# Layer 1's feed-forward: norm, stores, flips and the products of gate and up, regrouped

## The chip, the cores and the metric

The kernel runs on one core of a Trainium2 chip. The metric is the device time of one execution in microseconds (us). The engines are named as in the profile: PE is TensorE, DVE is VectorE, ACT is ScalarE, POOL is GpSimd, and SP is SyncE, which issues the stores here. In the trace each engine runs its own instructions in the order in which the built program has them, and waits at an instruction whose inputs are not there yet.

## The reference

The whole is a decoder of two layers on x of 4 x 512 rows of 512 columns. Each layer has a self-attention, a cross-attention and a feed-forward, and each of the six is followed by a norm:

```python
def _layernorm(x, axis=-1, eps=1e-05):
    m = jnp.mean(x, axis=axis, keepdims=True)
    v = jnp.var(x, axis=axis, keepdims=True)
    return (x - m) / jnp.sqrt(v + eps)
```

The change concerns the last of the six, layer 1's feed-forward, with weights of three values and inputs quantised to 8 bits by row:

```python
def _quant_act(x):
    s = jnp.max(jnp.abs(x), axis=-1, keepdims=True) / 127.0 + EPS
    xq = jnp.clip(jnp.round(x / s), -128.0, 127.0)
    return (xq, s)

def _qlinear(x, w):
    wq, ws = _quant_weight(w)
    xq, xs = _quant_act(x)
    y = jnp.einsum('bsi,oi->bso', xq, wq)
    return y * xs * ws
gate = jax.nn.silu(_qlinear(x, w_gate))
up = _qlinear(x, w_up)
return _qlinear(gate * up, w_down)
...
x = _layernorm(x + _L1_ffn_ref(x, L1_ffn_w_gate, L1_ffn_w_up, L1_ffn_w_down), axis=-1)
```

The inner width is 2048. The output is the result of that last norm.

## The kernel before, in words

x stays in SBUF as 16 tiles X[0] to X[15] of 128 rows by 512 columns; four tiles are one batch. The stages follow each other, and the feed-forward of layer 1 (`l1_ffn`) is the last. Its weights have been quantised and loaded as bf16 in the stage before, which also gives the scales `sg`, `su` and `sd` of the three weights as columns of one value per row.

`pipelined` runs `first(t)` for a tile, and after it `second(t - 1)` for the tile before.

`first(t)` finds the row's largest value (L1391), makes its scale `s` and the inverse (L1392, L1394), scales and rounds by adding a large constant (L1395, on DVE) and takes the constant off again into bf16 (L1396, on ACT). `flipped` turns the 128 x 512 values by four PE transposes into one PSUM tile (L1402), which DVE copies to SBUF (L1403). Then, for four pieces of 512 inner columns, PE makes gate's and up's products (`mm`, L160: four matmuls each, into `ps_s` and `ps_m`), ACT applies Silu to gate's (L1420), and DVE multiplies by up's (L1421). This gives four tiles `h` of 128 x 512.

`second(t, h)` takes the maximum of each `h` (L1427) and of the four (L1428), makes scale and inverse (L1429, L1430), quantises each piece (L1433 on DVE, L1434 on ACT) into `hq`, flips it by four groups of four transposes with four DVE copies (L1403), multiplies by the down weights (16 matmuls of L160 into one PSUM tile), and adds the result to X[t] (L1441, on DVE, the "residual" below).

After the fourth tile of a batch, `layernorm` takes mean and variance of its four tiles (`tile_moments`, L219 and L220 on DVE), the inverse root by ACT's Sqrt and a DVE reciprocal (`table_roots`, L243, L244), normalises the four tiles (`normalise_tile`, L239 on DVE), and SP stores them (L1445). Sqrt and Silu are in different tables of ACT, so that each batch has two loads of a table (ACT_TABLE_LOAD on L243 and L1420).

`inverse_roots` (L227 to L234) is the other way to the inverse root: a first guess from the bits of the number and three Newton steps, 15 small operations on POOL. Before the change it serves three batches of the cross-attention before, for four tiles at once.

Nothing in this stage writes the order of instructions out by hand. A scheduler puts each engine's instructions in order when the program is built, within what data, buffers and priorities allow; so the order on an engine isn't that of the source, and two tiles are mixed on every engine. Buffers here: three PSUM tiles each for `ps_s` and `ps_m`, two for `ps_t`; four `tmp` in SBUF, shared by the quantised x and Silu's outputs; eight tiles of h, which is two rows of tiles; one `hq` and one `hqt`.

Of the kernel before, what the change touches and what calls it, by code (L numbers as in the profile page):

```python
# [10 lines left out]
BF16 = mybir.dt.bfloat16  # L11
I32 = mybir.dt.int32
AF = mybir.ActivationFunctionType
ALU = mybir.AluOpType
AX = mybir.AxisListType
PSUM = bass.MemoryType.PSUM

P = 128
# [10 lines left out]
LN_EPS = 1e-05  # L29
Q_EPS = 1e-05  # L30
MASK_NEG = -2.3819763e38
ROOT_GUESS = float(0x5F3759DF)
ROUND = 12582912.0
# [53 lines left out]
def decoder_kernel(ctx: ExitStack, tc: tile.TileContext, a: dict, out: bass.AP):  # L87
    nc = tc.nc
# [20 lines left out]
    V, A, G, PE = nc.vector, nc.scalar, nc.gpsimd, nc.tensor  # L109


    def act(tag, free, bufs=1, dtype=F32):
        return ap.tile([P, *free], dtype, tag=tag, name=tag, bufs=bufs)

    def tmp(dtype=F32):
        return tp.tile([P, 512], dtype, tag="tmp", name="tmp")

    def small(n, tag, bufs=2):
        return sp.tile([P, n], F32, tag=tag, name=tag, bufs=bufs)

    def prob(tag, free, bufs, dtype=F32):
        return pools["pp"].tile([P, *free], dtype, tag=tag, name=tag, bufs=bufs)

    def pss():
        return pools["ps_s"].tile([P, 512], F32, tag="s", name="ps_s")

    def pst(dtype=F32):
        if "ps_t" not in pools:
            return psm(dtype)
        return pools["ps_t"].tile([P, 512], dtype, tag="t", name="ps_t")  # L130

    def psm(dtype=F32):
        return pools["ps_m"].tile([P, 512], dtype, tag="m", name="ps_m")
# [16 lines left out]
    def tk(t):  # L150
        return slice(t * P, (t + 1) * P)
# [4 lines left out]
    def mm(ps, lhs, rhs):  # L156

        n = len(lhs)
        for i, (x, y) in enumerate(zip(lhs, rhs)):
            PE.matmul(ps, lhsT=x, rhs=y, start=(i == 0), stop=(i == n - 1))  # L160
# [29 lines left out]
    X = []  # L190
    for t in range(T // P):
        x = xp.tile([P, F], F32, tag=f"x{t}", name=f"x{t}")
# [18 lines left out]
    moments = {}  # L211

    def tile_moments(b, i):

        if i == 0:
            moments[b] = small(8, "mv"), small(4, "rstd")
        mv = moments[b][0]
        st = sp.tile([P, 6], F32, tag="bn", name="bn")
        V.bn_stats(st, X[4 * b + i])  # L219
        V.bn_aggr(mv[:, 2 * i:2 * i + 2], st)  # L220

    def inverse_roots(b):


        mv, y = moments[b]
        v, t = small(4, "var"), small(4, "newton")
        G.tensor_scalar(v, mv.rearrange("p (t s) -> p t s", s=2)[:, :, 1], LN_EPS, None, ALU.add)  # L227
        G.tensor_scalar(y.bitcast(I32), v.bitcast(I32), -0.5, ROOT_GUESS, ALU.mult, ALU.add)
        G.tensor_scalar(v, v, -0.5, None, ALU.mult)
        for _ in range(3):  # L230
            G.tensor_tensor(t, v, y, ALU.mult)
            G.tensor_tensor(t, t, y, ALU.mult)
            G.tensor_scalar(t, t, 1.5, None, ALU.add)
            G.tensor_tensor(y, y, t, ALU.mult)  # L234

    def normalise_tile(b, i):
        mv, rstd = moments[b]
        x = X[4 * b + i]
        V.tensor_scalar(x, x, mv[:, 2 * i:2 * i + 1], rstd[:, i:i + 1], ALU.subtract, ALU.mult)  # L239

    def table_roots(b):
        mv, rstd = moments[b]
        A.activation(rstd, mv.rearrange("p (t s) -> p t s", s=2)[:, :, 1], AF.Sqrt, bias=LN_EPS)  # L243
        V.reciprocal(rstd, rstd)  # L244

    def layernorm(b):
        for i in range(4):
            tile_moments(b, i)
        table_roots(b)
        for i in range(4):  # L250
            normalise_tile(b, i)
# [46 lines left out]
    def pipelined(heads, first, second):  # L298

        held = None  # L300
        for h in heads:
            got = first(h)
            if held is not None:
                second(*held)
            held = (h, got)
        second(*held)
# [8 lines left out]
    def chunks(w):  # L315
        return [w[:, k, :] for k in range(w.shape[1])]
# [764 lines left out]
    def l1_xattn():  # L1081
# [163 lines left out]
        def out_projection(b, t, half, part):  # L1245

            if part == 0:
                kept["ps"] = psm()
            ps, n = kept["ps"][:, :256], slice(256 * half, 256 * half + 256)
            for k in range(2 * part, 2 * part + 2):  # L1250
                PE.matmul(ps, lhsT=fts[b][k][:, tk(t)], rhs=st["wo"][:, k, n],  # L1251
                          start=(k == 0), stop=(k == 3))
            if part == 0:
                return
            x = X[4 * b + t][:, n]
            V.tensor_tensor(x, x, ps, ALU.add)
            if half == 1:
                tile_moments(b, t)
            if (t, half) == (3, 1):
                (table_roots if b == B - 1 else inverse_roots)(b)  # L1260
# [123 lines left out]
    def l1_ffn():  # L1384
        wg, sg = quant["L1_ffn_gateT"]
        wu, su = quant["L1_ffn_upT"]
        wd, sd = quant["L1_ffn_downT"]

        def quantize(x, scratch, xq, s):

            V.tensor_reduce(s, x, AX.X, ALU.max, apply_absolute_value=True)  # L1391
            V.tensor_scalar(s, s, 1.0 / 127.0, Q_EPS, ALU.mult, ALU.add)  # L1392
            inv = small(1, "one", 8)
            V.reciprocal(inv, s)  # L1394
            V.tensor_scalar(scratch, x, inv, ROUND, ALU.mult, ALU.add)  # L1395
            A.activation(xq, scratch, AF.Copy, bias=-ROUND)  # L1396

        def flipped(dst, src, n):
            for c in range(n // 4):
                pt = pst(BF16)  # L1400
                for i in range(4):
                    PE.transpose(pt[:, tk(i)], src[:, tk(4 * c + i)], identb)  # L1402
                V.tensor_copy(dst[:, 4 * c:4 * c + 4, :], pt.rearrange("p (k n) -> p k n", k=4))  # L1403

        def first(t):
            s = small(1, "one", 8)
            xq, xqt = tmp(BF16), prob("q", [4, P], 3, BF16)
            quantize(X[t], tmp(), xq, s)
            flipped(xqt, xq, 4)
            gs, us = small(1, "one", 8), small(1, "one", 8)  # L1410
            V.tensor_tensor(gs, s, sg, ALU.mult)
            V.tensor_tensor(us, s, su, ALU.mult)
            h = [prob("P", [512], 8) for _ in range(4)]
            for n in range(4):
                pg, pu = pss(), psm()
                nn = slice(512 * n, 512 * n + 512)
                mm(pg, chunks(xqt), [w[:, nn] for w in wg])
                mm(pu, chunks(xqt), [w[:, nn] for w in wu])
                g = tmp()
                A.activation(g, pg, AF.Silu, scale=gs)  # L1420
                V.scalar_tensor_tensor(h[n], pu, us, g, ALU.mult, ALU.mult)  # L1421
            return h

        def second(t, h):
            part, s, inv = small(4, "part4"), small(1, "one", 8), small(1, "one", 8)
            for n in range(4):
                V.tensor_reduce(part[:, n:n + 1], h[n], AX.X, ALU.max, apply_absolute_value=True)  # L1427
            V.tensor_reduce(s, part, AX.X, ALU.max)  # L1428
            V.tensor_scalar(s, s, 1.0 / 127.0, Q_EPS, ALU.mult, ALU.add)  # L1429
            V.reciprocal(inv, s)  # L1430
            hq = prob("v", [4, 512], 1, BF16)
            for n in range(4):
                V.tensor_scalar(h[n], h[n], inv, ROUND, ALU.mult, ALU.add)  # L1433
                A.activation(hq[:, n, :], h[n], AF.Copy, bias=-ROUND)  # L1434
            hqt = act("attnT", [16, P], dtype=BF16)
            flipped(hqt, hq.rearrange("p n c -> p (n c)"), 16)
            po = psm()
            mm(po, chunks(hqt), wd)
            ds = small(1, "one", 8)
            V.tensor_tensor(ds, s, sd, ALU.mult)  # L1440
            V.scalar_tensor_tensor(X[t], po, ds, X[t], ALU.mult, ALU.add)  # L1441
            if t % 4 == 3:
                layernorm(t // 4)
                for i in range(4):
                    nc.sync.dma_start(out[tk(t - 3 + i), :], X[t - 3 + i])  # L1445

        pipelined(range(T // P), first, second)

    l1_ffn()


# [49 lines left out]
```

## Time and profile before

| | us |
|---|---|
| median of 3 runs | 2916.74 (2912.76 to 2916.99) |
| the profiled execution, its time | 2925.97 |
| its span | 2924.2 |
| mean granted PE clock | 0.983 |
| PE busy | 2763.2 (94%) |
| DVE busy | 1757.1 (60%) |
| ACT busy | 1046.8 (36%) |
| POOL busy | 425.0 (15%) |
| the feed-forward of layer 1 | 2704.9 to 2924.2 |
| in it: PE, DVE, ACT, POOL busy | 190.27, 195.11, 98.94, 0.00 |

The span is one profiled execution. A row of the timeline has start, duration (for several merged instructions from the first one's start to the last one's end), engine, line, operation, output and input, and the number of instructions; in brackets the idle time before it and who ended it. A row of the groups has total busy time, mean duration in ns, and the idle time before. A row of the chain of waits has start and length of a piece of the path that ended last. A row of the engines' busy time in a stretch has the stretch, its length, then busy time (and instructions) of PE, PE's weight loads, DVE, ACT and POOL, and then the clock, the DMA engines' share and GB/s.

### The profile page before, as it was taken

Reading aid. Unit: us, or ns where it says so; the run is one execution under the profiler, and the core shown is the slowest. Engines: PE = TensorE matmul, PEld = TensorE weight load, DVE = VectorE, ACT = ScalarE, POOL = GpSimd, SP = SyncE. Lnnn points to the kernel's source line nnn. Section 1 sums busy time; section 2 is a strip of 40 time slices with the busy share of each in tenths; the row PEclk is TensorE's granted clock in tenths of the full one; section 3 lists DMA queues with packets and bytes.
Section 4 is the critical chain, followed back from the end, with each engine's and each line's share of the span. In section 5 each row is a group of like instructions: output and inputs, shape, how many; then the busy total and the mean of one; then the engine's idle time right before and its main releaser. Section 6 shows DMA issues by size and latency. Waiting matters only on the chain. (4 is left out here: it accounts for less than half of the span.)

```text
span 2924.2 us, 30438 instructions
## 1 busy us (share of the span) xinstructions
PE 2763.2 (94%) x11434; PEld 1347.8 (46%) x11434; DVE 1757.1 (60%) x3551; ACT 1046.8 (36%) x1929; POOL 425.0 (15%) x436
## 2 busy tenths in 40 slices
PE   8999999998998889999999999999999999998987
PEld 3444444565665345555555555553334334334443
DVE  4565564553111476767667666756656666565998
ACT  2333342333221122232233223234555554554443
POOL 3000000042002100111101101123333232211000
PEclk9999999999999899999999999999999999999999
DMA  9700000004322120000000001111111020010000
GB/s 386 278 15 1 15 4 27 23 29 137 101 85 97 35 87 1 1 0 1 1 1 1 1 0 44 58 47 38 56 55 58 37 86 27 12 51 1 15 15 30
DMA packets 61128, 142.76 MB, mean 49 GB/s; under 512 B 6537, under 2 KB 26010, under 8 KB 54818
## 3 DMA queue, kind: packets, MB, share of 16 engines
q1 hardware_dynamic: 54818, 123.80, 11.8%
q0 software_dynamic: 6144, 16.79, 1.6%
q8 instruction: 99, 1.62, 0.2%
q14 instruction: 67, 0.55, 0.1%
HBM read 84.73 MB, written 47.45 MB: 45 GB/s over the span
## 5 line engine op out<-in xcount | busy, mean ns | idle before, releaser
L1182 DVE TENSOR_REDUCE maxes<-ps_b 128x2 f32<-128x1024 f32 x256 | 312.6, 1223 | 212.0 <-PE ps_b L1194 113.8
L160 PE MATMUL ps_m<-w,attnT 128*128 128x512 f32 (+1 forms) x992 | 391.8, 547 | 9.7 <-DVE x L313 9.7
L1198 ACT ACTIVATE PT<-ps_b 128x1024 f32<-128x1024 f32 x256 | 260.3, 1023 | 237.0 <-PE ps_b L1194 236.9
L1178 PE MATMUL ps_b<-k,q 32*128 32x512 f32 x1024 | 287.0, 642 | 6.8 <-ACT PT L1198 6.8
L1194 PE MATMUL ps_b<-q,k 32*128 32x512 f32 x1024 | 285.5, 642 | 1.4 <-DVE maxes L1182 1.4
L933 PE MATMUL ps_m<-xT,w 128*128 128x512 f32 x512 | 261.4, 594 | 0.0
L313 DVE TENSOR_TENSOR x<-x,ps_m 128x512 f32<-128x512 f32 x128 | 87.8, 687 | 284.5 <-PE ps_m L160 257.1
L160 PEld LDWEIGHTS ps_m<-w,attnT 128*128 128x128 f32 x736 | 141.2, 195 | 177.3 <-issue 162.8
L950 ACT ACTIVATE P<-ps_s,nmax 128x512 f32<-128x512 f32 (+3 forms) x256 | 135.4, 529 | 234.9 <-DVE nmax L948 233.8
L946 PE MATMUL ps_s<-k,q 128*128 128x512 f32 (+3 forms) x512 | 183.3, 441 | 19.1 <-POOL q L906 17.4
L906 POOL TENSOR_TENSOR q<-tmp 128x512 f32<-128x512 f32 x64 | 82.0, 1281 | 765.8 <-DVE tmp L905 731.2
L978 PE MATMUL ps_m<-PT,v 128*128 128x512 f32 (+3 forms) x512 | 162.8, 441 | 4.0 <-DVE PT L966 4.0
L370 ACT ACTIVATE P<-ps_s,nmax 128x512 f32<-128x512 f32 x128 | 88.5, 693 | 203.5 <-DVE nmax L368 203.5
L957 DVE TENSOR_SCALAR P<-P,sums 128x512 f32<-128x512 f32 (+3 forms) x256 | 152.0, 594 | 5.3
L1178 PEld LDWEIGHTS ps_b<-k,q 32*128 32x128 f32 x1024 | 76.5, 183 | 155.2 <-issue 141.1
L160 PE MATMUL ps_m<-w,xT 128*128 128x512 f32 (+1 forms) x384 | 143.8, 530 | 3.4 <-DVE v L338 3.4
L1205 PE MATMUL ps_m<-PT,vv 128*32 128x512 f32 x1024 | 137.5, 609 | 7.5 <-ACT PT L1198 7.5
L963 PEld LDWEIGHTS ps_t<-kc,P 128*128 128x128 f32 x640 | 84.0, 141 | 121.3 <-issue 82.0
L978 PEld LDWEIGHTS ps_m<-PT,v 128*128 128x128 f32 x512 | 89.0, 190 | 106.1 <-issue 48.8
L348 PE MATMUL ps_m<-xT,w 128*128 128x512 f32 x256 | 122.3, 605 | 10.4 <-DMA w<-in_L_attn_Wq 10.4
L948 DVE TENSOR_REDUCE nmax<-ps_s 128x1 f32<-128x512 f32 (+3 forms) x256 | 125.5, 490 | 5.6
L947 DVE TENSOR_TENSOR ps_s<-ps_s,mask 128x128 f32<-128x128 f32 x256 | 75.1, 294 | 81.1 <-PE ps_s L946 78.9
(281 smaller groups left out, 4403.7 us busy)
## 6 DMA issues: line engine op xcount, KB each, us to landing
hidden<-w SPq DMA_DIRECT2D x16, 1024.0 KB, 16.7
result<-w SPq DMA_DIRECT2D x16, 1024.0 KB, 16.3
w<-in_L_ffn_gateT SPq DMA_DIRECT2D x8, 1024.0 KB, 4.8
tmp<-tmp POOLq DMA_DIRECT2D x64, 128.0 KB
w<-in_L_ffn_upT SPq DMA_DIRECT2D x8, 1024.0 KB, 4.8
w<-in_L_ffn_downT SPq DMA_DIRECT2D x8, 1024.0 KB, 5.5
w<-in_L_attn_Wqkv SPq DMA_DIRECT2D x6, 1024.0 KB, 8.9
w<-in_L_attn_Wo SPq DMA_DIRECT2D x5, 1024.0 KB, 13.6
```

Source lines behind the costliest of these rows:

```text
L160: PE.matmul(ps, lhsT=x, rhs=y, start=(i == 0), stop=(i == n - 1))
L933: PE.matmul(ps_q[n], lhsT=wq[h // 4][:, i, tk(h % 4)], rhs=st["xt"][:, i, :], start=(i == 0), stop=(i == 3))
L946: PE.matmul(s[:, :w], lhsT=q[:, tk(qi)], rhs=k[:, :w], start=True, stop=True)
L948: V.tensor_reduce(nmax[:, qi:qi + 1], s[:, :w], AX.X, ALU.max, negate=True)
L950: A.activation(p[:, :w], s[:, :w], AF.Exp, bias=nmax[:, qi:qi + 1], accum_out=sums[:, qi:qi + 1])
L957: V.tensor_scalar(p[:, :w], p[:, :w], sums[:, qi:qi + 1], None, ALU.mult)
L978: PE.matmul(av[:, c * P:], lhsT=st["v"][:, c, tk(g)], rhs=pts[c][:, c * P:], start=(c == 0), stop=(c == 3))
L1178: PE.matmul(s[:, j, :], lhsT=q[strip(i), tk(qi)], rhs=k[strip(i), :], start=True, stop=True)
L1182: V.tensor_reduce(at[:, 2 * half:2 * half + 2, 16 * (1 - g % 2)], s, AX.X, ALU.max, negate=True)
L1194: PE.matmul(s[:, j, :], lhsT=k[strip(i), tk(c)], rhs=q[strip(i), :], start=True, stop=True)
L1198: A.activation(p, s, AF.Exp)
L1205: PE.matmul(avs[g][strip(i), :], lhsT=vv[c][:, 4 * m + i, 16 * par:16 * par + 32], rhs=pts[g, c, i // 2][:, i % 2, :], start=(c == 0), sto ...
```

## The change

- The norm is made tile by tile at the end of `second`, with `inverse_roots` on POOL for one column in place of `table_roots` for four; the tile is stored right after it.
- `flipped` is told which engine makes each copy: ACT for the quantised x, ACT and DVE in turn for the four copies of `hq`.
- `h` is two tiles of 128 x 1024 in place of four of 128 x 512: the maxima and the quantisation run over 1024 columns. The products by PE, Silu and the multiplication stay at 512.
- The products of `s` with `sg` and `su` are one operation on two columns (`both`, filled once in the stage before).

```diff
-    def inverse_roots(b):
-        mv, y = moments[b]
-        v, t = small(4, "var"), small(4, "newton")
-        G.tensor_scalar(v, mv.rearrange("p (t s) -> p t s", s=2)[:, :, 1], LN_EPS, None, ALU.add)
+    def inverse_roots(b, tiles=slice(0, 4)):
+        mv, y = moments[b][0], moments[b][1][:, tiles]
+        v, t = small(4, "var")[:, tiles], small(4, "newton")[:, tiles]
+        G.tensor_scalar(v, mv.rearrange("p (t s) -> p t s", s=2)[:, tiles, 1], LN_EPS, None, ALU.add)
...
-        def quantize(x, scratch, xq, s):
-            V.tensor_reduce(s, x, AX.X, ALU.max, apply_absolute_value=True)
-            V.tensor_scalar(s, s, 1.0 / 127.0, Q_EPS, ALU.mult, ALU.add)
-            inv = small(1, "one", 8)
-            V.reciprocal(inv, s)
-            V.tensor_scalar(scratch, x, inv, ROUND, ALU.mult, ALU.add)
-            A.activation(xq, scratch, AF.Copy, bias=-ROUND)
-        def flipped(dst, src, n):
+        both = small(2, "both", 1)
+        V.tensor_copy(both[:, 0:1], sg)
+        V.tensor_copy(both[:, 1:2], su)
+        def flipped(dst, src, n, copy_of):
             for c in range(n // 4):
                 pt = pst(BF16)
                 for i in range(4):
                     PE.transpose(pt[:, tk(i)], src[:, tk(4 * c + i)], identb)
-                V.tensor_copy(dst[:, 4 * c:4 * c + 4, :], pt.rearrange("p (k n) -> p k n", k=4))
+                copy_of[c](dst[:, 4 * c:4 * c + 4, :], pt.rearrange("p (k n) -> p k n", k=4))
+        def scale_of(s):
+            inv = small(1, "one", 8)
+            V.tensor_scalar(s, s, 1.0 / 127.0, Q_EPS, ALU.mult, ALU.add)
+            V.reciprocal(inv, s)
+            return inv
         def first(t):
-            s = small(1, "one", 8)
+            s, x, scratch = small(1, "one", 8), X[t], tmp()
             xq, xqt = tmp(BF16), prob("q", [4, P], 3, BF16)
-            quantize(X[t], tmp(), xq, s)
-            flipped(xqt, xq, 4)
-            gs, us = small(1, "one", 8), small(1, "one", 8)
-            V.tensor_tensor(gs, s, sg, ALU.mult)
-            V.tensor_tensor(us, s, su, ALU.mult)
-            h = [prob("P", [512], 8) for _ in range(4)]
+            V.tensor_reduce(s, x, AX.X, ALU.max, apply_absolute_value=True)
+            V.tensor_scalar(scratch, x, scale_of(s), ROUND, ALU.mult, ALU.add)
+            A.activation(xq, scratch, AF.Copy, bias=-ROUND)
+            flipped(xqt, xq, 4, (A.copy,))
+            scales = small(2, "scales")
+            V.tensor_scalar(scales, both, s, None, ALU.mult)
+            h = [prob("h", [2, 512], 4) for _ in range(2)]
             for n in range(4):
...
-                A.activation(g, pg, AF.Silu, scale=gs)
-                V.scalar_tensor_tensor(h[n], pu, us, g, ALU.mult, ALU.mult)
-            return h
+                A.activation(g, pg, AF.Silu, scale=scales[:, 0:1])
+                V.scalar_tensor_tensor(h[n // 2][:, n % 2, :], pu, scales[:, 1:2], g, ALU.mult, ALU.mult)
+            return [x.rearrange("p k n -> p (k n)") for x in h]
         def second(t, h):
-            part, s, inv = small(4, "part4"), small(1, "one", 8), small(1, "one", 8)
-            for n in range(4):
-                V.tensor_reduce(part[:, n:n + 1], h[n], AX.X, ALU.max, apply_absolute_value=True)
+            part, s, ds = small(2, "part2"), small(1, "one", 8), small(1, "one", 8)
+            for i in range(2):
+                V.tensor_reduce(part[:, i:i + 1], h[i], AX.X, ALU.max, apply_absolute_value=True)
             V.tensor_reduce(s, part, AX.X, ALU.max)
-            V.tensor_scalar(s, s, 1.0 / 127.0, Q_EPS, ALU.mult, ALU.add)
-            V.reciprocal(inv, s)
-            hq = prob("v", [4, 512], 1, BF16)
-            for n in range(4):
-                V.tensor_scalar(h[n], h[n], inv, ROUND, ALU.mult, ALU.add)
-                A.activation(hq[:, n, :], h[n], AF.Copy, bias=-ROUND)
+            inv = scale_of(s)
+            hq = prob("v", [2, 1024], 1, BF16)
+            for i in range(2):
+                V.tensor_scalar(h[i], h[i], inv, ROUND, ALU.mult, ALU.add)
+                A.activation(hq[:, i, :], h[i], AF.Copy, bias=-ROUND)
             hqt = act("attnT", [16, P], dtype=BF16)
-            flipped(hqt, hq.rearrange("p n c -> p (n c)"), 16)
+            flipped(hqt, hq.rearrange("p n c -> p (n c)"), 16, (A.copy, V.tensor_copy) * 2)
             po = psm()
             mm(po, chunks(hqt), wd)
-            ds = small(1, "one", 8)
             V.tensor_tensor(ds, s, sd, ALU.mult)
             V.scalar_tensor_tensor(X[t], po, ds, X[t], ALU.mult, ALU.add)
-            if t % 4 == 3:
-                layernorm(t // 4)
-                for i in range(4):
-                    nc.sync.dma_start(out[tk(t - 3 + i), :], X[t - 3 + i])
+            b, i = t // 4, t % 4
+            tile_moments(b, i)
+            inverse_roots(b, slice(i, i + 1))
+            normalise_tile(b, i)
+            nc.sync.dma_start(out[tk(t), :], X[t])
```

## The prediction

> **What bounds the kernel now.** I read the page first, then the feed-forward alone: its chain of waits, the busy time of the engines in one tile, and the timeline of VectorE (DVE). The page:
>
> ```profile
> span 2924.2 us, 30438 instructions
> ...
> PE   8999999998998889999999999999999999998987
> ...
> DVE  4565564553111476767667666756656666565998
> ```
>
> The change touches the last three slices (73 us each). There DVE is at 9, 9 and 8 tenths, and TensorE (PE) falls to 9, 8, 7. The feed-forward begins with the first gate product at 2704.93 us and ends with the span: 219.3 us. The chain of waits gives the start of gate's products by tile:
>
> ```profile
> 2740.55 1.04 PE ps_s L160 x4
> ...
> 2753.46 1.04 PE ps_s L160 x4
> ...
> 2793.21 1.04 PE ps_s L160 x4
> ...
> 2845.73 1.04 PE ps_s L160 x4
> ...
> 2898.24 1.04 PE ps_s L160 x4
> ```
>
> A plain tile takes 12.91 us (first two lines); four tiles with their batch's norm take 52.5 (third to fourth, fourth to fifth), 13.13 each. One plain tile by engine:
>
> ```profile
> 2740.55:2753.46 12.91, 11.97 (x69) 5.80 (x69) 11.83 (x31) 5.68 (x9) 0.00 (x0) 1.00 0.00 0
> ```
>
> PE is busy 11.97 of 12.91 us and DVE 11.83; ScalarE (ACT) has 7.2 us to spare, GpSimd (POOL) does nothing, the clock is 1.00. PE's gaps are waits for DVE ("PE ps_s <- DVE q" and the like). So DVE's strict order sets the pace, with PE close behind: at most about 0.9 to 1.1 us per tile can be gained.
>
> The operations that the change uses:
>
> ```profile
> 2713.21 1.86 DVE L1427 TENSOR_REDUCE part<-P 128x1 f32<-128x512 f32 x3
> ...
> 2908.25 1.67 DVE L1433 TENSOR_SCALAR P<-P,one 128x512 f32<-128x512 f32 x4
> ...
> 2917.24 1.92 DVE L239 TENSOR_SCALAR x<-x,mv,rstd 128x512 f32<-128x512 f32 x4
> ...
> L1044 DVE TENSOR_REDUCE part<-w 128x1 f32<-128x1024 f32 x24 | 28.9, 1205 | 0.0
> ...
> L968 ACT COPY PT<-ps_t 128x512 f32<-128x512 f32 x64 | 37.3, 583 | 114.9 <-PE ps_t L963 114.9
> ...
> 2289.24 0.18 DVE L220 BATCH_NORM_AGGREGATE mv<-bn 128x2 f32<-128x6 f32 x1
> ...
> 2289.52 0.23 POOL L227 TENSOR_SCALAR var<-mv 128x4 f32<-128x4 f32 x1 [16.19 <-DVE one L1049]
> ...
> 2289.83 0.19 POOL L228 TENSOR_SCALAR rstd<-var 128x4 int32<-128x4 int32 x1
> ...
> 2293.61 0.20 POOL L234 TENSOR_TENSOR rstd<-rstd,newton 128x4 f32<-128x4 f32 x1
> ```
>
> In a row of DVE instructions each duration overlaps the next by about 0.08 us (three reductions of 0.68 take 1.86), so a step below is duration less 0.08. The last lines are the Newton chain, here for four tiles at once and off the path: 15 POOL operations from 2289.52 to 2293.81, 4.29 us, a step of 0.286 although each lasts 0.2. It starts 0.10 after the aggregate ends.
>
> **The change part by part, per tile.**
>
> - Flips: five PSUM-to-SBUF copies on DVE become two; three go to ACT. DVE saves 3 x 0.33 = 1.0. ACT pays 3 x 0.58 (nearest row: its 128x512 copy from PSUM, 583 ns), and lies at about 7.2 busy in a tile of 13 to 14.
> - h in two pieces of 1024: four reductions (4 x 0.60) become two of 1.205 (2 x 1.13): 0.15 saved. Four scalings (4 x 0.40) become two; the row of that shape (L1062, 128x1024) says 754 ns: 2 x 0.66, 0.28 saved. The price is grain: ACT's first half of hq takes 1.06 (L1064, 1057 ns) instead of 0.62.
> - gs and us in one operation: 0.1 saved. The two copies into `both` sit in the cross attention, where DVE idles for PE: nothing (0.3 us if that cover went).
> - Norms: Sqrt, its reciprocal and two table loads per batch go away; 15 POOL operations of one column per tile come in. Stores leave tile by tile from SP, which has nothing else queued and is not on the path until the last one.
>
> DVE's work sinks from about 12.5 us per tile to 10.6. What decides is where the program puts the waiting instruction. In the compiled order of the changed kernel, DVE runs for each tile: residual (the `scalar_tensor_tensor` into X[t], L1441 before), bn_stats, aggregate, **one** product of gate and up (L1421 before), then the normalisation (L239) of the tile just aggregated, which waits for POOL; and queued behind it on DVE are the other three products, both maxima of h, the next tile's quantisation, two flip copies, both scalings of h and the next residual. PE and ACT wait for these.
>
> DVE's walk from L239 to the next aggregate, in steps: L239 0.46; product 0.70 (the maximum after it waits for its end); maximum 1.13; product 0.66 (two take 1.41 in the trace); quantising x 0.40; product 0.66; copy 0.33; maximum 1.14; copy 0.33; four small ones 0.51 (2725.01 to 2725.52 in the trace); maximum of x 0.60; two scalings 1.32; residual to end of aggregate 1.69 (0.79 from residual to bn_stats, 0.90 on to the end). Sum **9.93**. Then the Newton chain: 0.10 + 4.29 + 0.05 = **4.44**; the one product (0.70) lies inside it. Cycle **14.37 us** against 13.13.
>
> Are PE and ACT ready within that cycle? Count from L239's start. First scaling ends at 7.66; ACT's half of hq 8.8; ACT's copy of the next tile's q 9.4; gate's products start at 9.5 and take 6.9 of PE, so they end 2.0 into the next cycle, before the flips are asked for at 4.0. The down product needs DVE's last copy (5.9) and then eight products and latency: ready at about 8.0, asked for at 8.25. It fits, with 0.2 to spare; where it doesn't, up to 0.4 per tile comes on top.
>
> The chain's length for one column instead of four: below, 15 x (0.10 + 0.085) = 2.8, if an operation cost only what a POOL memset of 128x1 costs (102 ns); above, 4.29 plus one blocked operation, 4.7. I take 4.29: the 45 operations of 128x4 in the trace all last 0.19 to 0.23 but one, and on 128x512 an operation takes 1.28, which makes three columns worth about 6 ns.
>
> Two rules weighed. First, the one operation that stands out: L227 took 634 ns once (else 217 to 228), while DVE ran L1062, a scaling from SBUF to SBUF, until 2654.54; it ended at 2654.62. The Trainium skill (SBUF — State Buffer, Who interferes with whom) has the rule: DVE in a two-port mode and GpSimd exclude each other, and the second waits for the whole instruction. This speaks against putting 240 POOL operations beside DVE: if one operation of each chain were caught so (+0.41), the cycle would be 14.8 and the sum 6 us more. But here, while the chain runs, DVE has only the product to do, whose one tensor input beside g is in PSUM; I add nothing and keep 6 us for the upper end.
>
> Second, the table loads: the trace has 1283 ns each, and all that DVE waited for Sqrt in the feed-forward is 4.8 us in five waits ("DVE rstd L244 <- ACT rstd L243"), one of which stays. The skill (ScalarE: Activation LUTs, What ACT_TABLE_LOAD costs) prices a switch at 2.66 us with its drain; eight switches fewer would be worth 21 us and all but cancel the loss below. ACT is idle over half the time here, so a load costs only what DVE waits. I go by the row: that gain is already in the 13.13 against 12.91.
>
> **The sum, by the start of gate's products.**
>
> - Tile 2: +1.9. Tile 1's quantisation now stands behind a maximum of 1.2 and the fourth product, its q copy goes over ACT (0.58 for 0.41), and tile 2's q copy stands on ACT behind both halves of hq.
> - Tile 3: +3.3. The first norm has not even a product in its cover (+0.7, and the first full wait).
> - Tile 4: +4.8 (14.4 against a plain 12.9).
> - Tiles 5 to 15: 11 x (14.37 - 13.13) = 13.6. Tile 15 stands at 2898.24 + 18.4 = 2916.6.
> - The end. Before, from tile 15's first product to the end 26.0 us. After: 4.9 to L239 of tile 13; 5.9 to the scalings (no quantisation is left); residual, bn and aggregate of tile 14 end 9.4 after that L239; its chain holds DVE to 13.8; normalisation, then tile 15's residual at 14.3, aggregate 16.0, chain 20.4, normalisation 20.9. Before, last normalisation to the end took 5.0 with four stores at once; with one of 256 KB I take 4.6. In all 4.9 + 20.9 + 4.6 = 30.4: +4.4.
>
> Sum 18.4 + 4.4 = **+22.8 us** on the profiled execution: span 2924.2 to 2947.0. That execution took 2925.97, 9 us above the median 2916.74 of the runs shown; the difference is carried to the median: **2939.5 us**, 0.8% slower. Runs of this kernel differ by about 0.15%; within 0.2% (6 us) I call no change.
>
> **Rivals.**
>
> 1. *Short Newton chain, faster.* For it: one column is less than four, and a 128x1 memset took 0.10. If the step were 0.12, the chain would be 1.9 us with its latencies, DVE's cycle 11.9, and PE's 11.97 the bound: 14 tiles x 1.1 = 15 less, the end 2 more: about 2904. It turns to a gain at a chain of about 3.0 us (22.8 shared over 16 chains is 1.4 less), a step under 0.2. Against it: the steps of 0.28 to 0.31 at four columns, three quarters of which is not data. 7%.
> 2. *PE and ACT add their own waits.* The 0.2 spare is gone, because hq comes in halves of 1.06 and ACT carries three copies in order between the Silus: 0.4 per tile, +6; with blocked POOL operations another 6: 2945 to 2951. For it: ACT's queue now stands in PE's path twice per tile. 20%.
> 3. *The wait is partly hidden.* Chain at 3.5 to 3.9, or DVE's walk shorter where durations overlap more: cycle 13.6 to 14.0, +10 to +17: 2927 to 2934. 15%. Nearer still to zero, no change: 5%.
>
> My forecast, the full chain in every tile, has the rest, 53%. All but rival 1 and the last 5% are slower: 0.88. The range reaches over 2 and 3: 2926 to 2951.
>
> **What would show it.** Right: L239 in the feed-forward waits for "POOL rstd L234", some 3.7 us sixteen times, over 55 us in all; POOL busy 45 to 50 us there in 240 operations of about 0.2; gate's products every 14.4 us with the batch's fourth tile like the others; DVE's busy time down by 25 to 30 us and yet a longer span; one table load in place of eight. Wrong: L239 waiting under 2.5 us, POOL's step under 0.2, or PE's products without gaps. If tiles come at more than 14.8, look at "DVE x <- PE ps_m" and at ACT's copies for rival 2.

## The result, and the profile after

| | before | after |
|---|---|---|
| median, same chip | 2916.23 us (4 runs) | 2940.01 us (4 runs, 2929.93 to 2944.28) |
| ratio | | 1.0079, 95% interval 1.0051 to 1.0106 |
| profiled execution: time, span | 2925.97, 2924.2 | 2929.93, 2928.2 |
| feed-forward, first gate product to the end | 219.27 us | 247.15 us |
| a tile's cycle | 12.91, with the norm 13.13 | 14.27 |

The changed kernel is slower by 23.8 us of the medians (15 to 31 by the interval). The two spans alone say only 4 us. The stages ahead of the feed-forward are the same code but for the two copies into `both`, and yet took 24 us less in this execution: the first gate product stands at 2681.0, and between 2687 and 2714 in the other executions below. So I read the change from the length of the feed-forward, **+27.9 us**, and check that against the ratios of whole runs.

The page after; three rows that answer to those of before:

```profile
span 2928.2 us, 30561 instructions
...
PE   8999999998998889999999999999999999997886
...
DVE  4565565553212577766766767656656666575775
```

DVE sinks from 9, 9, 8 tenths to 7, 7, 5 in the last three slices, and PE sinks too, to 8, 8, 6. Less work on the busiest engine, and more idle time on both. The chain of waits gives the starts of gate's products:

```profile
2735.64 1.04 PE ps_s L160 x4
...
2749.91 1.04 PE ps_s L160 x4
...
2835.54 1.04 PE ps_s L160 x4
...
2849.81 1.04 PE ps_s L160 x4
...
2892.10 1.04 PE ps_s L160 x4
```

Every tile takes 14.27 us, the batch's fourth tile like the others. One tile, then the whole stage (stretch, length, then busy time of PE, weight loads, DVE, ACT, POOL, then clock, DMA share, GB/s):

```profile
2835.54:2849.81 14.27, 11.98 (x68) 5.82 (x69) 10.69 (x24) 6.71 (x11) 2.95 (x15) 1.00 0.05 19
2681.01:2928.20 247.19, 193.25 (x1084) 93.11 (x1084) 172.35 (x366) 109.43 (x161) 47.23 (x240) 0.96 0.05 18
```

DVE's work is down by 22.7 us (195.08 to 172.35), POOL has 47.2 us in 240 operations, and no engine is over 84% busy in a tile. DVE's timeline at the head of one tile (start, duration, in brackets the idle time before and who ended it):

```profile
2821.73 0.18 DVE L220 BATCH_NORM_AGGREGATE mv<-bn 128x2 f32<-128x6 f32 x1
2823.27 0.75 DVE L1425 SCALAR_TENSOR_TENSOR h<-ps_m,scales,tmp 128x512 f32<-128x512 f32 x1 [1.36 <-ACT tmp L1424]
2826.14 0.55 DVE L239 TENSOR_SCALAR x<-x,mv,rstd 128x512 f32<-128x512 f32 x1 [2.12 <-POOL rstd L234]
2826.60 0.74 DVE L1425 SCALAR_TENSOR_TENSOR h<-ps_m,scales,tmp 128x512 f32<-128x512 f32 x1
```

From the aggregate's end (2821.91) to the normalisation (2826.14) pass 4.23 us. Only 0.75 of it is work; DVE waits 1.36 us for Silu and 2.12 us for POOL. Then the second product, whose operands are long there, and all the rest of the tile's list run without a gap until the next aggregate at 2836.0, 9.9 us after the normalisation's start.

### The profile page after: what moved, and what is told of

Its sections match the earlier page's. It is cut to its first block, busy times and chain, and to the rows that moved or that the text cites. A ratio compares the mean times of both kernels' runs of the same rounds, so it can differ in the third digit from the quotient of the medians.

```text
span 2928.2 us, 30561 instructions
## 1 busy us (share of the span) xinstructions
PE 2752.3 (94%) x11434; PEld 1342.5 (46%) x11434; DVE 1736.9 (59%) x3421; ACT 1055.8 (36%) x1934; POOL 470.2 (16%) x676
## 5 line engine op out<-in xcount | busy, mean ns | idle before, releaser
L160 PE MATMUL ps_m<-w,attnT 128*128 128x512 f32 (+1 forms) x992 | 385.4, 541 | 0.4 <-DVE attnT L1398 0.4
```

## The experiments

All are changes of the feed-forward alone. Each ratio is against runs of the kernel before on the same chip; "stage" is the time from the first gate product to the end in the profiled execution (before 219.3, after 247.2). My theory after the result had two parts: the normalisation stands one product behind its own aggregate in DVE's order, so each cycle is DVE's walk plus the Newton chain; and the end is late because POOL's closing DRAIN starts only after the last Newton step. The rival for the first part: ScalarE's copies and the coarser pieces slow the tile.

| kernel | stage, us | against before | ratio, 95% interval |
|---|---|---|---|
| norm only | 268.7 | +49.4 | 1.0167 (1.0151 to 1.0184) |
| all but the norm | 222.5 | +3.2 | 1.0012 (1.0001 to 1.0023) |
| last two tiles' Newton on DVE | 237.9 | +18.7 | 1.0058 (1.0046 to 1.0071) |
| before, with a late POOL copy | 223.5 | +4.3 | one run |
| normalisation two products later | 232.0 | +12.8 | 1.0047 (1.0028 to 1.0065) |
| no norm, rounding behind flip copy | 222.5 | +3.2 | 1.0016 (1.0003 to 1.0028) |
| pieces only | 228.9 | +9.6 | 1.0028 (1.0013 to 1.0043) |
| norm later, rounding later, Newton on DVE | 226.3 | +7.0 | 1.0028 (1.0016 to 1.0040) |
| no norm, input flipped early | 199.2 | -20.0 | 0.9929 (0.9909 to 0.9948) |
| before, input flipped early | 198.2 | -21.1 | 0.9920 (0.9901 to 0.9939) |
| input flipped early, norm by tile | 211.9 | -7.4 | 0.9970 (0.9958 to 0.9982) |

The stage's difference agrees with the ratio of whole runs within 2.3 us in each row that has one (0.0167 of 2928 us is 49, 0.0058 is 17, -0.0071 of 2912 is -21). It is 27.9 against 23.8, inside the interval, for the changed kernel.

**The norm alone.** The kernel before, with the new norm at the end of `second`:

```diff
-            if t % 4 == 3:
-                layernorm(t // 4)
-                for i in range(4):
-                    nc.sync.dma_start(out[tk(t - 3 + i), :], X[t - 3 + i])
+            b, i = t // 4, t % 4
+            tile_moments(b, i)
+            inverse_roots(b, slice(i, i + 1))
+            normalise_tile(b, i)
+            nc.sync.dma_start(out[tk(t), :], X[t])
```

> The kernel before with only the final norm of the changed kernel (each tile's moments, Newton's method on POOL, normalisation and store by themselves); flips on DVE alone and products in four pieces as before. Theory (the wait in VectorE's order): the tile's DVE work stays at about 12.5 us less the batch's share, and the wait for the Newton chain, 4.2 us as the changed kernel's trace has it, less some 1 us covered, is added to every tile: a cycle of 15.5 to 16.5 us where the kernel before has 12.91 to 13.13; feed-forward (first gate product to the end) 260 to 275 us against 219.3, some +40 to +55. Rival (the coarser pieces and ScalarE's flip copies are what slows the changed kernel): feed-forward within 222 to 230 us, +3 to +10 with the tail alone.

Measured: stage 268.7 us, and from tile 2 on tiles of 15.0 to 17.1 us. The kernel with the norm alone is 49 us slower; the rival is out as the main cause. Its chain of waits runs through POOL (start, length, piece):

```profile
2887.80 0.20 POOL rstd L234
2888.00 0.03 issue
2888.02 0.04 DVE x L239
```

But not all of the 49 us is the wait. Two tiles by engine (the eighth figure is the granted clock):

```profile
2754.30:2770.72 16.42, 13.50 (x69) 6.21 (x69) 12.26 (x32) 5.57 (x9) 2.95 (x15) 0.90 0.04 16
2770.72:2785.84 15.12, 11.98 (x68) 5.82 (x69) 12.17 (x32) 5.57 (x9) 2.95 (x15) 1.00 0.05 18
```

Of the 13 tiles from tile 2 to tile 14, nine are like the first, with 3.4 us of half TensorE clock in each, and four are like the second. Together the nine take 12 us more than nine tiles of 15.12 us would. So by this estimate some 12 us of the 49 came by way of the clock, and the cycle at full clock, 15.1 us, lies below the 15.5 that the theory had.

**All but the norm.** The same lines taken back in the changed kernel:

```diff
-            b, i = t // 4, t % 4
-            tile_moments(b, i)
-            inverse_roots(b, slice(i, i + 1))
-            normalise_tile(b, i)
-            nc.sync.dma_start(out[tk(t), :], X[t])
+            if t % 4 == 3:
+                layernorm(t // 4)
+                for i in range(4):
+                    nc.sync.dma_start(out[tk(t - 3 + i), :], X[t - 3 + i])
```

> The changed kernel with the norm as it was before: every fourth tile its batch is normalised from ScalarE's square roots and stored in four. The flip copies of two engines and the two pieces stay. Theory (the wait in VectorE's order): without it the tile's DVE work of 10.6 us no longer carries a chain; the cycle falls under 12.9 to between 11.5 and 12.5 us unless ScalarE or TensorE bind; feed-forward 200 to 213 us against 219.3 before, -6 to -19, and 35 to 45 us less than the changed kernel's 247.2. Rival (pieces and flip copies slow it): the cycle stays near 14 us, feed-forward 235 us or more.

Measured: stage 222.5 us, 13.17 per tile (12.79 each fourth), time +0.12%. I had expected 35 to 45 us less than in the changed kernel, and 6 to 19 less than before; it is 24.7 less, and 3.2 more. The norm, with its wait and its late end, accounts for 24.7 of the change's 27.9 us, which is most of it, as the theory says. But two pieces and flips on two engines, with 1.5 us less DVE work per tile (10.38 here against 11.88 in a tile of the kernel before), are not faster than before. The chain of waits of one tile shows why (from the last of the products on):

```profile
2862.93 0.88 PE ps_m L160 x4
...
2863.90 0.75 DVE h L1425
2864.65 0.33 DVE attnT L1398
2864.99 1.13 DVE part L1431
...
2867.55 0.67 DVE h L1436
...
2868.30 1.06 ACT v L1437
2869.36 0.48 ACT q L1398
2869.84 0.05 issue
2869.89 1.04 PE ps_s L160 x4
```

The last product, the maximum of the second piece, the scaling and ACT's rounding of the first piece, and only then ACT's copy of the next tile's q. It stands behind that rounding in ACT's order, and DVE had finished with the next input at 2863.5. So 7 us of products and 6 us of the rest are in series, however little DVE has to do.

**The end: Newton of tiles 14 and 15 on DVE, and a late POOL copy.** Two edits, one on each kernel:

```diff
-            inverse_roots(b, slice(i, i + 1))
+            inverse_roots(b, slice(i, i + 1), V if t >= 14 else G)
```

```diff
             if t % 4 == 3:
                 layernorm(t // 4)
+                if t == T // P - 1:
+                    G.tensor_copy(small(8, "late"), moments[t // 4][0])
```

> The changed kernel with the Newton steps of the last two tiles (14 and 15) on VectorE in place of POOL, all else alike. Theory for the end (the 10.8 us DRAIN of POOL's queue, which starts after POOL's last Newton step and which the end of the program waits for): POOL's last step is now that of tile 13, some 28 us earlier, its drain is over before the last store, and the time from the last normalisation to the end falls from 10.85 us to about 5, so -6 us; with the shorter chain of tile 15 and 14 (15 steps on VectorE at less each) -7 to -9 us in all. Rival (the end is late since the last tile's norm and store stand alone): the time from the last normalisation to the end stays at 10 to 11 us, and only the chain's 1 to 3 us are gained.

> The kernel before with one more POOL instruction, a copy of the last batch's moments (128x8) as soon as the last tile's moments are there; nothing waits for its result. Theory for the end (POOL's DRAIN starts after its last instruction and takes 10.8 to 11.9 us): the span ends some 11 to 12 us after this copy, the drain's row stands in the last 12 us of the span in place of starting at 2668, and the time from the last gate product to the end grows from 26.0 us to about 30 to 32. Rival (the drain's length is only what it waits for, or belongs to the Newton steps): the end stays at 26 us after the last tile's first gate product.

The row of POOL's closing DRAIN (count: shortest/middle/longest in ns, first and last start), in the kernel before, after, with the two tiles on DVE, and before with the late copy:

```profile
L1489 POOLq DRAIN  x3: 44/113/11867, 2668.4 to 2923.9; - x3
```

```profile
L1492 POOLq DRAIN  x3: 44/113/10783, 2916.5 to 2927.9; - x3
```

```profile
L1492 POOLq DRAIN  x3: 44/113/10785, 2924.2 to 2946.2; - x3
```

```profile
L1491 POOLq DRAIN  x3: 44/113/10767, 2913.1 to 2924.4; - x3
```

Its first start is just behind the issue of POOL's last instruction, and it takes 10.8 to 11.9 us. Before, it had ended 244 us ahead of the end. After, it starts at 2916.53, when the last Newton step is on its way, and the program ends at 2928.2, though the last tile was normalised at 2917.35 and its store lands 2 us after its issue at 2917.4. With two tiles' Newton on DVE the drain starts at 2924.2, 22 us ahead of the end: the stage is 9.2 us shorter than after, 1.9 of it in the chains and 7.3 from the last normalisation to the end (10.8 to 3.5 us). With the late copy in the kernel before, the span ends 11.4 us behind that copy, and the time from tile 15's first product to the end grows from 25.96 to 30.17 us. All four kernels that end on a POOL instruction of the norm, or on this copy, have 11.4 us from its end to the end of the span (after, norm only, late copy, normalisation two products later). So it is neither the Newton steps nor the single last store.

**The normalisation two products later.** The changed kernel, with one tile's normalisation and store emitted in the next tile's `second` and held behind the third product of its cycle on DVE (`third` keeps that instruction; `issue_after` sets the order within the engine; `...` marks lines left out):

```diff
+                if n == 2:
+                    third[t] = last.ins
...
+            if t > 0:
+                if t + 1 in third:
+                    with tc.issue_after(third[t + 1]):
+                        normalise_tile((t - 1) // 4, (t - 1) % 4)
...
+                nc.sync.dma_start(out[tk(t - 1), :], X[t - 1])
             tile_moments(b, i)
             inverse_roots(b, slice(i, i + 1))
-            normalise_tile(b, i)
-            nc.sync.dma_start(out[tk(t), :], X[t])
...
```

> The changed kernel with each tile's normalisation put two products later in VectorE's order, behind the third product of its cycle rather than the first, so that the Newton chain lies beside products; POOL's work, flips and pieces stay. Theory (VectorE waits for Newton's method because the normalisation stands one product behind its aggregate): the wait of 2.1 us for POOL goes, and the cycle falls from 14.27 us to that of the kernel with the batch norm, 13.2 to 13.4; 13 cycles give 12 to 14 us, the start (10.2 and 15.8) and the last tile's 36 us stay; from the first gate product to the end 233 to 236 us against 247.2. Rival (ScalarE and the coarser pieces set 14.27, the wait only fills time that is idle anyway): the cycle stays at 14.0 to 14.3.

Measured: 13.17 us in every tile, stage 232.0. DVE's waits for POOL, after, and here:

```profile
DVE x L239 <- POOL rstd L234: 39.1, 16, 4.2
```

```profile
DVE x L239 <- POOL rstd L234: 7.5, 2, 4.2
```

Sixteen waits become two, those of the last two tiles, and 14.27 becomes 13.17: the same POOL work and the same flips and pieces, in another place. This shows the first part of the theory. It also shows that 13.17 is the next bound, to the hundredth that of the kernel with the batch norm. And it bears on the table loads: from tile 0 to tile 15 that kernel has seven of them and this one has one, and they take 196.4 and 196.6 us. It is no clean price, as the normalisations stand in other places too, but no gain from six loads fewer shows.

**What binds at 13.17.** First the rounding behind the flip copy, on the kernel with the batch norm:

```diff
-                A.activation(hq[:, i, :], h[i], AF.Copy, bias=-ROUND)
+                if t + 1 in turned_x:
+                    with tc.issue_after(turned_x[t + 1]):
+                        A.activation(hq[:, i, :], h[i], AF.Copy, bias=-ROUND)
...
```

> The kernel with the batch norm, two pieces and flips on two engines (13.17 us per tile), with one order added: the rounding of a tile's two pieces on ScalarE is queued behind the flip copy of the next tile's input, which is ready some 4 us earlier. Theory (in that kernel the next tile's products wait for TensorE's flips of the pieces and for ScalarE's flip copy, which stand behind the first piece's rounding, so that last product, maximum, scaling, rounding and copy come in series, 6 us behind 7 us of products): the products start when the down product is through, and the cycle falls to 11.6 to 12.4 us, where TensorE's 11.8 us of work or VectorE's 10.4 bind; from the first gate product to the end 203 to 213 us against 222.5 and against 219.3 before. Rival (the cycle is held by VectorE's or ScalarE's total work with their hand-overs, not by this order): 13.0 us or more, 220 us.

A miss: 13.0 us in plain tiles, up to 13.6 with a norm. "Ready some 4 us earlier" was wrong: the next input was rounded that early, but its flips were not made. In the kernel without this edit they stand behind the down product on TensorE:

```profile
2865.17 2.75 PE L160 MATMUL ps_m<-w,attnT 128*128 128x512 bf16 x12
2867.76 0.39 PE L1397 MATMUL ps_t<-identb,tmp 128*128 128x128 bf16 x4
```

With the edit the q copy is no longer behind the rounding, but still behind these flips, as the chain of waits shows:

```profile
2865.25 3.24 PE ps_m L160 x15
2868.49 0.24 PE ps_t L1397 x4
2868.72 0.02 issue
2868.75 0.59 ACT q L1398
2869.34 0.05 issue
2869.39 0.82 PE ps_s L160 x3
```

All flips back on DVE, with the two pieces and the batch norm:

```diff
-            flipped(xqt, xq, 4, (A.copy,))
+            flipped(xqt, xq, 4, (V.tensor_copy,))
...
-            flipped(hqt, hq.rearrange("p n c -> p (n c)"), 16, (A.copy, V.tensor_copy) * 2)
+            flipped(hqt, hq.rearrange("p n c -> p (n c)"), 16, (V.tensor_copy,) * 4)
```

> The kernel with the batch norm and the two pieces, all flips copied by VectorE as before. VectorE's work per tile rises by three copies of 0.33 us to 11.4. Theory (the series of last product 0.75, flip copies 1.0, maximum 1.13, scalars 0.5, maximum of the next input 0.59, scaling 1.33, residual 0.66 and flip copy 0.33 follows 7.0 us of products): a cycle of 13.2 to 13.4 us, as with two engines or 0.2 longer: the two pieces alone gain nothing either. Rival (ScalarE's copies are what eats the gain of the pieces): 12.0 to 12.6 us.

Plain tiles take 13.09 us; two of each four, around the batch's norm, take 13.85 and 14.9; the stage is 9.6 us longer than before. The theory's plain cycle held roughly, its silence on the norm did not. Pieces alone lose; ScalarE's flip copies give back 6.4 us of it. The rival is out.

Then all at once: the normalisation later, the rounding later, and Newton on DVE for the last two tiles (against the changed kernel; the later normalisation as above):

```diff
-                A.activation(hq[:, i, :], h[i], AF.Copy, bias=-ROUND)
+                if t + 1 in turned_x:
+                    with tc.issue_after(turned_x[t + 1]):
+                        A.activation(hq[:, i, :], h[i], AF.Copy, bias=-ROUND)
...
-            inverse_roots(b, slice(i, i + 1))
+            inverse_roots(b, slice(i, i + 1), V if t >= 14 else G)
```

> All together: the changed kernel with the normalisation behind the third product of its cycle, the rounding queued behind the next tile's flip copy, and the Newton steps of tiles 14 and 15 on VectorE. Theory: the cycle of 14.27 us falls to 11.7 to 12.6 us (0.46 us of normalisation more on VectorE than with the batch norm, no wait for square roots), the end to 26 to 28 us since POOL's drain is covered; from the first gate product to the end 205 to 217 us against 247.2, and 2 to 14 us faster than the kernel before. Rival (the parts of the theory don't add up, ScalarE binds): 225 us or more.

13.46 us per tile, 226.3: the rival was right that the parts don't add up. The end is repaired (26.4 us from tile 15's first product), the cycle isn't. What sets 13.46 us is not shown here.

**The next input flipped early.** On the kernel with the batch norm and the later rounding, quantising and flips of x move into `prepare`, which is called a tile ahead, and the down product is held behind them:

```diff
-        def first(t):
+        def prepare(t):
...
+        def first(t):
+            if t == 0:
+                prepare(0)
+            if t + 1 < T // P:
+                prepare(t + 1)
+            xqt, scales = ready[t]
...
-            mm(po, chunks(hqt), wd)
+            with tc.issue_after(flips_x[min(t + 2, T // P - 1)]):
+                mm(po, chunks(hqt), wd)
```

> The kernel with the batch norm and the rounding behind the flip copy (13.0 to 13.6 us per tile), with one step more: each tile's input is quantised and flipped one tile earlier, and the down product on TensorE is queued behind the flips of the next input, so that the flip copy of 0.59 us on ScalarE and the flips of 0.24 us lie beside the down product of 3.5 us and no longer between it and the next products. Theory (in that kernel TensorE's chain of 6.9 products, 1.7 Silu, rounding and copy, 0.6 flips, 3.5 down, 0.8 flips and copy of the next input makes the cycle): the last 0.8 us goes and part of the 1.7, so 11.9 to 12.8 us per tile; from the first gate product to the end 206 to 219 us, 0 to 13 us faster than the kernel before. Rival (VectorE's order takes over again, since the maximum of a tile's second piece follows all its products): 13.0 us or more, no gain.

Measured: 11.7 to 12.0 us per tile from tile 2 on, stage 199.2, ratio 0.9929 (0.9909 to 0.9948): faster than both kernels, and by more than the theory had. Four tiles:

```profile
2773.26:2820.81 47.55, 46.70 (x275) 23.23 (x273) 43.02 (x94) 29.55 (x44) 0.00 (x0) 1.00 0.06 23
```

PE is busy 46.70 of 47.55 us. That is the bound that the kernel before had in view (11.97 of PE's work in 12.91) and could not reach.

**What flips and pieces are worth then.** The same `prepare` and the same hold on the down product in the kernel before, without any part of the change:

```diff
-        def first(t):
+        def prepare(t):
...
+            ready[t] = xqt, gs, us
...
+        def first(t):
+            if t == 0:
+                prepare(0)
+            if t + 1 < T // P:
+                prepare(t + 1)
+            xqt, gs, us = ready[t]
...
-            mm(po, chunks(hqt), wd)
+            with tc.issue_after(flips_x[min(t + 2, T // P - 1)]):
+                mm(po, chunks(hqt), wd)
```

> The kernel before (four pieces, all flips copied by VectorE, norm by batch) with only the order of the last experiment: each tile's input is quantised and flipped one tile earlier, and the down product is queued behind the flips of the next input. It tells what flips and pieces are worth once the order no longer binds. Theory (with the order free, VectorE's own work decides, 11.4 to 11.9 us per tile here against 10.4 with two pieces and flips on two engines): 12.2 to 12.9 us per tile, from the first gate product to the end 206 to 217 us, between the last experiment's 199.2 and the 219.3 of before. Rival (the order alone made the gain, flips and pieces none): under 12.0 us, 199 to 203 us.

A miss for my theory, a hit for the rival: 198.2 us and 0.9920 (0.9901 to 0.9939), not to be told from the last one. The larger part of the stage by engine:

```profile
2710.14:2845.87 135.73, 134.31 (x778) 66.62 (x793) 135.02 (x360) 68.05 (x111) 0.00 (x0) 1.00 0.04 16
```

Both PE and DVE are full (134.31 and 135.02 of 135.73 us; some PE records are missing from this trace, so I give no cycle by tile). DVE's larger work fits, and the order alone makes the gain. Which of its two parts does, the earlier input or the held down product, no run here tells apart.

**The norm by tile on top.** To the kernel of the last experiment but one (two pieces, `prepare`):

```diff
-            if t % 4 == 3:
-                layernorm(t // 4)
...
+                    with tc.issue_after(third[t + 1]):
+                        normalise_tile((t - 1) // 4, (t - 1) % 4)
...
+            inverse_roots(b, slice(i, i + 1), V if t >= 14 else G)
```

> The last experiment's kernel (11.85 us per tile) with the norm of the changed kernel, each tile's normalisation behind the third product of its cycle and the Newton steps of tiles 14 and 15 on VectorE. Theory (the norm tile by tile costs nothing by itself where the Newton chain of 4.2 us lies beside products and POOL's drain is covered): 11.8 to 12.2 us per tile, 197 to 205 us from the first gate product to the end, within 6 us of the last experiment. Rival (VectorE with the norm in each cycle, or the chain, binds again): 12.6 us or more, 211 us.

Again nearer the rival: 12.75 us per tile once it runs, and 211.9. In this order one product stands ahead of the aggregate, and only two behind it before the normalisation, so the chain shows again:

```profile
2816.48 0.17 DVE L220 BATCH_NORM_AGGREGATE mv<-bn 128x2 f32<-128x6 f32 x1
...
2820.90 0.55 DVE L239 TENSOR_SCALAR x<-x,mv,rstd 128x512 f32<-128x512 f32 x1 [0.92 <-POOL rstd L234]
2821.36 0.48 DVE L1415 TENSOR_SCALAR tmp<-x,one 128x512 f32<-128x512 f32 x1
```

The wait is only 0.92 us; but the quantising behind it (L1415) is what ACT's rounding and flip copy, PE's flips and the down product wait for in turn, and the chain of waits of this kernel runs through all fifteen POOL operations.

## Why the prediction was right, and where it was not

- **The order and the cycle: right.** L239 stands one product behind its aggregate; walk 9.93 and chain 4.44 were to give 14.37. Measured: 9.9 and 4.23, a cycle of 14.27. The experiment that moved L239 took the wait away and 1.10 us per tile with it, and the kernel with the norm alone showed the loss without flips and pieces.
- **The wait's size: wrong.** I wrote 3.7 us sixteen times, over 55 in all, and named a wait of under 2.5 us as a sign of error. It is 39.1 us, 2.4 each, and yet the mechanism stands: the one product "inside" the chain doesn't take 0.70 but 2.1 us, as it waits 1.36 for Silu. A wait by its row says who came last, not how long the chain is.
- **The start: 1.4 us too little.** Tiles 2, 3 and 4 came 3.3, 4.7 and 6.1 us later than before, not 1.9, 3.3 and 4.8. Tile 1's products ran at half TensorE clock for 3.4 us (last section) and took 8.8 us where a later tile's take 7.1; the sum had no term for that. No run takes the half clock away by itself, so its share of the 1.4 us is an estimate.
- **Tiles 5 to 15: 11.7 us for 13.6**, from the cycle 0.1 shorter and a last step of 13.75.
- **The end: the term that was mis-sized.** Predicted +4.4 us, measured 36.06 against 25.96, +10.1. The part up to the last normalisation held (25.2 for 25.8). The step that failed is the 4.6 us from the last normalisation to the end, taken from the 5.0 of before with its four stores: it is 10.8, since POOL's drain now starts last of all. I had counted POOL's instructions and not what POOL does once they are over.
- **The sum.** 22.8 - 1.9 + 1.4 + 5.7 = 28.0, the 27.9 of the trace. That the median came out at 2940.01 for 2939.5 is in part luck: the terms missed by up to 5.7 us, and the working carried the profiled execution's distance from the median over to another set of runs, whose interval allows 15 to 31 us.
- **The rivals.** The short chain is out: a step of 0.27 to 0.29 us at one column as at four. The prediction's count against it, that three quarters of a step is not data, was too low: by its own 2 ns a column, a step of 286 ns at four columns holds about 8 ns of data. And the rival's price was wrong: without any wait the cycle doesn't fall to PE's 11.97 but to 13.17, no gain over 12.91, because the order on ACT and PE binds there. ACT's order in PE's path, my second rival, did not add to 14.27; it stood 1.1 us under it and was the next bound.
- **DVE's work: a sign that missed.** It sank by 22.7 us, not by 25 to 30. The gains that the prediction lists come to 1.5 us a tile, 24.5 in all; its "about 12.5" before was too high, as 195.1 us over 16 tiles are 12.2. Nothing in the sum hung on it.
- **The two rules.** No POOL operation was blocked: the longest of the 240 took 227 ns, and I had added nothing for it. Seven table loads went, not eight (one of the stage's eight stays), and no gain of 2.66 us each, the price that the prediction weighed and set aside, shows: the kernel with the batch norm keeps its loads and reaches the same 13.17 us.

## What to carry to other kernels

Where two tiles are mixed on in-order engines, draw the cycle through the orders of all engines before counting an engine's busy time. Here 1.5 us less work on the busiest engine bought nothing, while preparing the next tile's input one tile earlier and holding the down product behind its flips bought 0.8% of the whole time. Put the reader of a slow side chain behind work that is as long as the chain, or the chain becomes part of the cycle, and ask again after every reordering. At the end of a program, see which engine's last instruction comes late: what that engine does when it closes is then no longer hidden.

## What the runs showed of the hardware that I had not expected

- **POOL closes slowly.** Its DRAIN at the end of the program takes 10.77 to 10.79 us behind an operation of 0.19 us, and 11.87 behind the one of 1.27 us in the kernel before: 10.6 us from the end of the last operation. The other engines' take 0.01 to 4.5 us. The four kernels here that end on POOL pay it; those whose last POOL operation lies 19.6 us or more ahead of the end do not.
- **A short gap can halve the TensorE clock.** In the changed kernel PE idles 2.09 us ahead of tile 1's flips and 0.68 behind them. Busy time and clock (the eighth figure is the granted clock) in stretches of 1 us:

```profile
2688.24:2689.24 1.00, 0.00 (x0) 0.00 (x0) 1.00 (x3) 0.00 (x0) 0.00 (x0) 1.00 0.00 0
...
2691.24:2692.24 1.00, 1.00 (x4) 0.39 (x5) 1.00 (x2) 0.00 (x0) 0.00 (x0) 0.66 0.00 0
2692.24:2693.24 1.00, 1.00 (x4) 0.42 (x3) 0.82 (x2) 0.30 (x1) 0.00 (x0) 0.50 0.00 0
2693.24:2694.24 1.00, 1.00 (x4) 0.30 (x2) 0.00 (x0) 1.00 (x2) 0.00 (x0) 0.50 0.00 0
2694.24:2695.24 1.00, 1.00 (x4) 0.40 (x3) 0.59 (x1) 1.00 (x2) 0.00 (x0) 0.63 0.00 0
2695.24:2696.24 1.00, 1.00 (x7) 0.46 (x5) 0.51 (x4) 0.73 (x2) 0.00 (x0) 1.00 0.00 0
```

Read as shares of half and full clock, that is 3.4 us at half. Tile 1's step is 15.8 us where the kernel before, with gaps of 0.43 and 0.52 us there and a clock of 1.00 throughout, has 14.3; it is 14.8 to 15.8 in the five other kernels with this gap, which all drop to half clock there, and 14.2 with the pieces alone, which has no such gap. The Trainium skill (TensorE: Matmul & The Clock Gate, What's actually happening) puts the return to half clock at an idle window of about 3.4 us or more; here 2.8 us of idle with 0.4 us of transposes between were enough. The measurement decides. The length of the gap is not the whole of it: with the norm alone PE idles 2.2 us or more in one piece in each of the 13 tiles above, and the clock fell in nine of them, at 1.2 to 1.3 us a tile in all but the first; what sets the four others apart is open.
